# Last attention block of a two-layer convolutional attention kernel: denominators on 64 rows, reciprocals from PSUM, and the range check split over the last two blocks

## The chip, the core and the metric

The kernel runs on one core of one Trainium2 chip. The metric is the device time of one execution in microseconds; the time of a kernel is the median of its runs. A profile is one execution recorded by the hardware profiler.

The engines in what follows: PE is TensorE (PEld its weight loads), DVE is VectorE, ACT is ScalarE, POOL is GpSimd, and SP issues most DMAs (SPq is its queue). An engine runs its own instructions in program order, and waits on semaphores for the others.

## The reference

Input x is (16, 256, 32, 32) in float32: 16 images with 256 channels and n = 1024 positions. Two layers, each with weights of its own, do the same:

```
def layer(x, Wq, bq, Wk, bk, Wv, bv, rel_h, rel_w):
    xf = _gn(x).reshape(b, c, n)           # groups of two columns of the last axis, mean and variance over channels too
    q, k, v = (proj(W, bias) for ...)      # 256 x 256, then 4 heads of d = 64
    sim  = einsum('bhdi,bhdj->bhij', q, k)
    rel  = (rel_h + rel_w).reshape(heads, d, n)
    qpos = einsum('hdi,bhdj->bhij', rel, q)
    attn = softmax(sim + qpos, axis=-1)
    return einsum('bhdn,bhmn->bhdm', v, attn)

x = x + layer(x, L0...)
x = x + layer(x, L1...)
```

Two terms make the logits: sim, and the position term qpos. The softmax needs, for each head and each query i, the sum of 1024 exponentials: the denominator. The division by it is done after the product with v.

## The kernel before

**Tiling.** A unit is one image in one layer (32 units, the two layers interleaved). Its four heads are worked on as two pairs `pr`; a pair fills 128 partitions, 64 for each head. The 1024 queries are cut into two halves of 512. So there are 32 x 2 x 2 = 128 blocks (unit, pair, half), numbered 0 to 127. A block walks over eight slices `j` of 128 keys. With keys on the partitions, the logits of one slice are a PSUM tile of 128 x 2 x 512: two heads, 512 queries.

**One slice.** `seed` (L332) lets VectorE write the position terms into the PSUM tile: the products of rel with q were made once for each pair (`positions`, L309), and the seed adds the part of rel_h and the part of rel_w with broadcasts. `scores` (L348) adds the product of k and q on top with four matmuls of 64 x 64 x 512 (the trace has two records for each). They are quadrants of the array: the head picks the 64 rows, the half of the slice's keys picks the 64 columns. ACT takes the exponential into SBUF (L357). `add_up` (L366, L368) adds the eight results on VectorE into `acc`, so that `acc` still has to be summed over its 128 partitions.

**The rest of a block.** `attend` (L382) multiplies v with the exponentials into a PSUM tile `po`, in two stretches with a word from POOL (L152) between them. In the second half of a pair, `sums_of_p` (L405) sums the two `acc` of the pair over the partitions with matmuls against ones; each of the four (half, head) gets 32 rows of `po`. `take_out` copies `po` to SBUF (`od`; L417 in the first half, L422 in the second), and four DMAs (L431) take one row of each sum into `den_all`, where a block's denominators stand as 128 x 8. In the next block, `reciprocals` (L439) inverts them as 128 x 16, writes them to DRAM (L442) and reads them back, broadcast over 64 partitions a head, as `rden` (L445). `finish` multiplies (L456), adds bias and x (L457), and in layer 1 sends the result to `out` (L459).

**Order.** The whole is written under a manual schedule: each engine gets its instructions in the order of the program text. `block(n)` writes out that order by hand. Four PSUM tiles of two banks, `ring` = b, c, a, d, rotate; the seeds of slices 1 to 3 of the next block are made at the end of a block, between the stretches of `attend`. While a block runs, the projections, normalisation and position terms of the coming unit are put between its slices as `pieces` (`first`, `second`). The last two blocks, 126 and 127, have no such pieces.

**The end.** After block 127 come `reciprocals` and `finish` for the last pair. Then, outside the manual schedule, a pool of its own checks that every denominator lies between 1e-22 and 1e24: two operations and a reduction over `den_all` as 128 x 1024 (L969, L971, L973), a matmul that counts the good partitions (L975), and a cast to an integer (L977). The program reads this flag and branches: if a partition is out of range, a slow general path computes everything anew. The exponentials use a fixed shift instead of a maximum, which is why the check is there.

Of the kernel before, what the change touches and what calls it, by code (L numbers as in the profile page):

```python
# [9 lines left out]
F32 = mybir.dt.float32  # L10
F32R = mybir.dt.float32r
I32 = mybir.dt.int32
AF = mybir.ActivationFunctionType
ALU = mybir.AluOpType
AX = mybir.AxisListType
SYNC = mybir.DependencyInfo(mybir.DependencyClass.Sync, mybir.DependencyReason.DATA)

P = 128
HALF = 512
# [5 lines left out]
DEN_LO = 1e-22  # L25
# [18 lines left out]
def flat(ap):  # L44
    return ap.rearrange("p w h -> p (w h)")
# [4 lines left out]


@with_exitstack
def fast_path(ctx, tc, sh, x, layers, out, W, den_all, token):

# [282 lines left out]
        )  # L339
        seeds[blk, j] = ps  # L340

    def scores(blk, j):
        u, pr, half = blk
        ps = seeds.pop((blk, j))
        for h, hs in enumerate(QUARTERS):
            for x, c in enumerate(QUARTERS):
                j0 = j * P + x * D
                nc.tensor.matmul(  # L348
                    ps[c, h, :],
                    ks[u, pr][hs, j0 : j0 + D],  # L350
                    qs[u, pr][hs, half * HALF : (half + 1) * HALF],
                    start=False,
                    stop=True,
                    skip_group_check=True,
                )
        p = ppool.tile([P, 2, HALF], F32, tag="p", name=f"p_{u}_{pr}_{half}_{j}")
        nc.scalar.activation(p, ps, AF.Exp, bias=W.shift)  # L357
        probs[blk, j] = p
# [53 lines left out]
    def take_out(blk, po):  # L412

        u, pr, half = blk
        if half == 0:
            outs[u, pr] = opool.tile([P, 3, HALF], F32, tag="od", name=f"od_{u}_{pr}")
            nc.scalar.copy(  # L417
                outs[u, pr][:, 0, :].rearrange("p (a n) -> p a n", a=2), po[:, :, :QUART]
            )
            return  # L420
        od = outs[u, pr]
        nc.scalar.copy(  # L422
            od[:, 1:3, :].rearrange("p z (a n) -> p z a n", a=2),
            po.rearrange("p a (z n) -> p z a n", z=2),
        )
        R = P // 4
        n = index[blk]
        for x in range(2):
            for h in range(2):
                r0 = (2 * x + h) * R  # L430
                nc.sync.dma_start(  # L431
                    den_all[h * D : (h + 1) * D, n - 1 + x, :], od[r0 : r0 + 1, 2, :]
                )

    def reciprocals(u, pr):

        n = index[u, pr, 0]
        r8 = fpool.tile([P, 2, 8], F32, tag="r8", name=f"r8_{u}_{pr}")
        nc.vector.reciprocal(r8, den_all[:, n : n + 2, :])  # L439
        rd = dpool.tile([2, 2, HALF], F32, tag="rd", name=f"rd_{u}_{pr}")  # L440
        for x in range(2):
            nc.sync.dma_start(rd[:, x, :].rearrange("h (a b) -> h a b", b=8), r8[:, x, :])  # L442
        rdens[u, pr] = opool.tile([P, 2, HALF], F32, tag="rden", name=f"rden_{u}_{pr}")
        for h in range(2):
            nc.sync.dma_start(  # L445
                rdens[u, pr][h * D : (h + 1) * D],
                rd[h : h + 1].to_broadcast([D, 2, HALF]),
            )

    def finish(u, pr):  # L450
# [8 lines left out]
            nc.sync.dma_start(flat(out[b, pr * P : (pr + 1) * P]), xs)  # L459


    blocks = [(u, pr, half) for u in range(NU) for pr in range(CC) for half in range(NH)]
    for n, blk in enumerate(blocks):
        index[blk] = n
    BPU = CC * NH

    ring = ["b", "c", "a", "d"]

    def nothing(*_):
# [28 lines left out]
    def block(n):  # L498
        blk = blocks[n]
        u, b = divmod(n, BPU)  # L500
        half = blk[2]
        before = blocks[n - 2][:2] if half == 0 and n > 0 else None
        after = blocks[n + 1] if n + 1 < len(blocks) else None
        one, two = u + 1 < NU, u + 2 < NU

        pieces = u + 1 < NU or b < 2
        f0, f1, f2, f3 = ring

        if half == 1:
            add_up(blocks[n - 1], 7)  # L510
        for j in range(1, 4):
            scores(blk, j)
        if b == 2 and u + 3 < NU and units[u + 3][0] not in xt:
            load_x(units[u + 3][0])
        (first, first_out), (second, second_out) = prepare(u, b)
        first(0)
        if b == 0 and one:
            norm_apply(u + 1, range(0, 1))
        if b == 1 and two:
            norm_sums(u + 2, range(9, 11))  # L520
        seed(blk, 4, f1)
        scores(blk, 4)
        add_up(blk, 1)
        if half == 0:
            if before:
                reciprocals(*before)
            add_up(blk, 2)
        if b == 0 and one:
            norm_apply(u + 1, range(1, 5))
        if b == 1 and two:  # L530
            norm_sums(u + 2, range(11, 12))
        if b == 2 and two:
            norm_squares(u + 2, range(0, 5))
        second(0)
        if half == 1:
            second_out()
        first(1)
        first_out()
        seed(blk, 5, f0)
        scores(blk, 5)  # L540
        if half == 0:
            add_up(blk, 3)
            second(1)
            second_out()
        seed(blk, 6, f1)
        scores(blk, 6)
        if pieces and half == 0:
            ring[2:] = f3, f2
        seed(blk, 7, ring[2])
        scores(blk, 7)  # L550
        if half == 1:
            add_up(blk, 2)
            add_up(blk, 3)
        add_up(blk, 4)

        if after:
            seed(after, 0, f0)
        if before:
            finish(*before)
        if b == 0 and one:  # L560
            norm_apply(u + 1, range(5, 9))
        if b == 0 and two:
            norm_sums(u + 2, range(0, 2))
        if b == 1 and two:
            norm_sums(u + 2, range(12, G))
        if b == 1 and one:
            norm_apply(u + 1, range(9, 11))
        if b == 2 and two:
            norm_squares(u + 2, range(5, 11))
        po = psum2(ring[3], f"po_{n}")  # L570
        values_of_p = attend(blk, po)
        values_of_p(0)
        if two and half == 1:
            mean, mean_out = (norm_mean if b == 1 else norm_var)(u + 2, zeroed(f1, f"pm_{n}"))
            mean(0)
        if after:
            scores(after, 0)
        if two and half == 1:
            mean(1)
            values_of_p.word()  # L580
            mean_out()
        add_up(blk, 5)
        if half == 1:
            add_up(blk, 6)
            add_up(blk, 7)
        if after:
            for j in range(1, 4):
                seed(after, j, ring[j % 3])
        if half == 0:
            add_up(blk, 6)  # L590
        if b == 0 and two:
            norm_sums(u + 2, range(2, 9))
        if b == 1 and one:
            norm_apply(u + 1, range(11, G))
        if b == 2 and two:
            norm_squares(u + 2, range(11, G))
        values_of_p(1)
        if half == 1:
            sums_of_p(blocks[n - 1 : n + 1], po)
        take_out(blk, po)  # L600


    load_x(0)
# [107 lines left out]
    seed(blocks[0], 3, ring[0])  # L711
    for n in range(len(blocks)):
        block(n)
    reciprocals(*blocks[-1][:2])
    finish(*blocks[-1][:2])


@with_exitstack
# [224 lines left out]
def kernel(  # L943
# [10 lines left out]
    nblk = sh.NL * sh.B * sh.CC * sh.NH  # L954
    den_all = const.tile([P, nblk, 8], F32, tag="den_all", name="den_all")
    token = const.tile([1, 1], F32, tag="token", name="token")
    with tc.manual_schedule():
        W = Weights(tc, sh, layers, const)
        fast_path(tc, sh, x, layers, out, W, den_all, token)


    with ExitStack() as s:
        pool = s.enter_context(tc.tile_pool(name="chk", bufs=1))
        psum = s.enter_context(
            tc.tile_pool(name="chk_ps", bufs=1, space=bass.MemoryType.PSUM)
        )
        flatden = den_all.rearrange("p n e -> p (n e)")
        low = pool.tile([P, nblk * 8], F32, tag="low", name="low")
        nc.vector.tensor_scalar(low, flatden, DEN_LO, None, ALU.is_ge)  # L969
        good = pool.tile([P, nblk * 8], F32, tag="good", name="good")  # L970
        nc.vector.scalar_tensor_tensor(good, flatden, DEN_HI, low, ALU.is_le, ALU.mult)  # L971
        cnt = pool.tile([P, 1], F32, tag="cnt", name="cnt")
        nc.vector.tensor_reduce(cnt, good, AX.X, ALU.min)  # L973
        pc = psum.tile([P, 1], F32, tag="pc", name="pc")
        nc.tensor.matmul(pc[0:1, :], cnt, W.ones[:, 0:1], start=True, stop=True)  # L975
        flag = const.tile([1, 1], I32, tag="flag", name="flag")
        nc.vector.tensor_copy(flag, pc[0:1, :])  # L977
    ok = nc.values_load(flag[0:1, 0:1], min_val=0, max_val=P)
    with tc.If(ok < P):
        general_path(tc, sh, x, layers, out, W)  # L980
# [30 lines left out]
```

## Time and profile before

| what | value |
|---|---|
| median of three runs | 2654.65 us (2654.4 to 2658.43) |
| the profiled execution | 2655.58 us |
| its span on the core | 2652.5 us |
| mean granted TensorE clock | 0.995 |
| chain that ended last, by engine | PE 84%, DVE 6%, DMA 6%, SP's queue 2% |
| PE waiting at L348 for the seeds, all blocks | 15.1 us |
| VectorE waiting at L439 for den_all, all pairs | 39.6 us |
| VectorE waiting at L456 for rden, all pairs | 31.8 us |

The span is what the trace shows on the core; around it lie 3.1 us of the profiled execution. Busy times are sums over the span and can hide that stages have different limits, so the last 70 us are read by slices and by the timeline. A row of the timeline has the start, the duration, the engine, the line of the kernel, the operation, output<-input with shapes, the count, and in brackets the idle time ahead of it with what ended it. Rows of the groups have busy time, mean duration of one in ns, and the idle time ahead of the group with what ended it.

### The profile page before, as it was taken

Reading aid. Unit: us, or ns where it says so; the run is one execution under the profiler, and the core shown is the slowest. Engines: PE = TensorE matmul, PEld = TensorE weight load, DVE = VectorE, ACT = ScalarE, POOL = GpSimd, SP = SyncE. Lnnn points to the kernel's source line nnn. Section 1 sums busy time; section 2 is a strip of 40 time slices with the busy share of each in tenths; the row PEclk is TensorE's granted clock in tenths of the full one; section 3 lists DMA queues with packets and bytes.
Section 4 is the critical chain, followed back from the end, with each engine's and each line's share of the span. In section 5 each row is a group of like instructions: output and inputs, shape, how many; then the busy total and the mean of one; then the engine's idle time right before and its main releaser. Section 6 shows DMA issues by size and latency. Waiting matters only on the chain.

```text
span 2652.5 us, 86141 instructions
## 1 busy us (share of the span) xinstructions
PE 2591.0 (98%) x38406; PEld 1389.7 (52%) x38406; DVE 2423.2 (91%) x2198; ACT 1980.2 (75%) x3916; POOL 176.5 (7%) x450
## 2 busy tenths in 40 slices
PE   7999999999999999999999999999999999999994
PEld 3555555555555555555555555555555555555552
DVE  6999999999999999999999999999999999999996
ACT  5778777787777787777877777877778777778652
POOL 1000000000000000000000000000000000000000
PEclk9999999999999999999999999999999999999997
DMA  2010010101001010010100101001010100000001
GB/s 74 11 33 18 26 34 19 34 26 34 26 19 42 18 42 18 18 50 10 42 26 10 50 18 34 26 26 34 19 34 27 34 26 19 26 18 26 26 26 34
DMA packets 61499, 75.48 MB, mean 28 GB/s; under 512 B 43200, under 2 KB 44736, under 8 KB 61120
## 3 DMA queue, kind: packets, MB, share of 16 engines
q1 hardware_dynamic: 59664, 69.83, 9.1%
q8 instruction: 302, 4.95, 0.8%
q14 instruction: 77, 0.63, 0.1%
q10 hardware_dynamic: 1456, 0.07, 0.0%
HBM read 52.04 MB, written 17.30 MB: 26 GB/s over the span
## 4 chain that ended last, share of the span: by engine, by line
PE 84%; DVE 6%; DMA 6%; SPq 2%; issue 1%; ACT 1%; POOL 0%; DVEq 0%; POOLq 0%
PE po L382 30%; PE ps L348 29%; PE pv L281 7%; PE pq L251 7%; PE pk L251 7%; DVE ps L332 3%; PE po L405 2%; DMA rd<-r 2%; DMA rden<-rd 2%; PE pa L309 2%; DVE acc L368 2%; DMA den_all<-od 1%; SPq L431 1%; DVE x L457 1%; DVE od L456 1%
## 5 line engine op out<-in xcount | busy, mean ns | idle before, releaser
L357 ACT ACTIVATE p<-ps,shift 128x1024 f32<-128x1024 f32 x1024 | 1092.3, 1114 | 337.4 <-PE ps L348 215.4
L332 DVE TENSOR_TENSOR ps<-abt 128x1024 f32<-128x1024 f32 x1024 | 1228.7, 1228 | 112.3 <-ACT p L357 94.1
L348 PE MATMUL ps<-q,k 64*64 64x512 f32 x8192 | 997.5, 593 | 15.5 <-DVE ps L332 15.1
L368 DVE TENSOR_TENSOR acc<-acc,p 128x1024 f32<-128x1024 f32 x768 | 933.7, 1216 | 16.1 <-DVE r L439 0.2
L382 PE MATMUL po<-p,v 64*64 64x256 f32 x16384 | 933.1, 376 | 0.3 <-POOL token L152 0.3
L382 PEld LDWEIGHTS po<-p,v 64*64 64x64 f32 x16384 | 668.3, 133 | 294.6 <-issue 60.4
L348 PEld LDWEIGHTS ps<-q,k 64*64 64x64 f32 x8192 | 299.1, 133 | 443.3 <-issue 273.3
L251 PE MATMUL pq<-xn,Wq 64*64 64x512 f32 x2048 | 244.3, 592 | 4.0 <-DVE xn L640 4.0
L281 PE MATMUL pv<-Wv,xn 64*64 64x256 f32 x4096 | 244.3, 376 | 1.6 <-POOL token L152 1.3
L251 PE MATMUL pk<-xn,Wk 64*64 64x512 f32 x2048 | 242.8, 589 | 0.0
L231 ACT ACTIVATE xn<-x,nshift,rstd 128x128 f32<-128x128 f32 x501 | 213.4, 501 | 1.6 <-POOL nshift L654 1.6
L281 PEld LDWEIGHTS pv<-Wv,xn 64*64 64x64 f32 x4096 | 153.6, 133 | 103.3 <-issue 51.1
L176 ACT ACTIVATE junk<-x,neg 128x128 f32<-128x128 f32 x489 | 191.7, 399 | 0.0
L152 POOL MEMSET token<- 1x1 f32 x380 | 33.8, 89 | 2360.2 <-PE po L382 657.9
L422 ACT COPY od<-po 128x1024 f32<-128x1024 f32 x64 | 64.8, 1012 | 152.1 <-PE po L405 152.1
L366 DVE TENSOR_TENSOR acc<-p,p 128x1024 f32<-128x1024 f32 x128 | 155.9, 1218 | 0.0
L251 PEld LDWEIGHTS pq<-xn,Wq 64*64 64x64 f32 x2048 | 78.5, 134 | 145.6 <-issue 133.0
L176 ACT ACTIVATE junk<-x 128x128 f32<-128x128 f32 x480 | 144.9, 311 | 0.7 <-DVE x L457 0.7
L251 PEld LDWEIGHTS pk<-xn,Wk 64*64 64x64 f32 x2048 | 75.4, 133 | 124.2 <-issue 124.2
L220 POOL TENSOR_TENSOR rstd<-var,mhalf 128x16 f32<-128x16 f32 x30 | 113.2, 3773 | 59.1 <-ACT var L218 59.1
L456 DVE TENSOR_TENSOR od<-od,rden 128x1024 f32<-128x1024 f32 x64 | 78.2, 1221 | 31.9 <-DMA rden<-rd 31.8
L291 ACT COPY v<-pv 128x1024 f32<-128x1024 f32 x64 | 64.8, 1012 | 48.1 <-PE pv L281 48.1
(59 smaller groups left out, 921.1 us busy)
## 6 DMA issues: line engine op xcount, KB each, us to landing
rden<-rd SPq DMA_DIRECT2D x128, 256.0 KB
x<-in_x_dram SPq DMA_DIRECT2D x32, 512.0 KB
out_dram<-x SPq DMA_DIRECT2D x32, 512.0 KB
den_all<-od SPq DMA_DIRECT2D x256, 2.0 KB
rd<-r SPq DMA_DIRECT2D x128, 4.0 KB
raw<-in_L_conv_Wq_dram SPq DMA_DIRECT2D x2, 256.0 KB
raw<-in_L_conv_Wk_dram SPq DMA_DIRECT2D x2, 256.0 KB
raw<-in_L_conv_Wv_dram SPq DMA_DIRECT2D x2, 256.0 KB
```

Source lines behind the costliest of these rows:

```text
L176: nc.scalar.activation(junk, grouped(xt[units[u][0]], g), func, accum_out=into[:, g : g + 1], **bias)
L220: nc.gpsimd.tensor_tensor(rstd, var, W.mhalf[:, :G], ALU.pow)
L231: nc.scalar.activation(grouped(xns[u], g), grouped(xt[units[u][0]], g), AF.Identity, bias=shift[:, g : g + 1], scale=rstd[:, g : g + 1],)
L251: yield nc.tensor.matmul(pk[c, nh, :], w[l][rs, cc, c0 : c0 + D], xns[u][rs, cc, nh * HALF : (nh + 1) * HALF], start=(t == 0 and cc == 0), ...
L281: yield nc.tensor.matmul(pv[c, a, i, :], xns[u][rs, cc, j0 : j0 + D], W.wv[l][rs, cc, :], start=(t == 0 and cc == 0 and i == 0), stop=(t = ...
L332: nc.vector.tensor_tensor(ps.rearrange("p h (w y) -> p h w y", y=H), ab[:, :, :H].unsqueeze(2).to_broadcast([P, 2, XH, H]), ab[:, :, H + h ...
L348: nc.tensor.matmul(ps[c, h, :], ks[u, pr][hs, j0 : j0 + D], qs[u, pr][hs, half * HALF : (half + 1) * HALF], start=False, stop=True, skip_g ...
L357: nc.scalar.activation(p, ps, AF.Exp, bias=W.shift)
L366: nc.vector.tensor_tensor(accs[blk], probs[blk, 0], probs[blk, 1], ALU.add)
L368: nc.vector.tensor_tensor(accs[blk], accs[blk], probs[blk, j], ALU.add)
L382: yield nc.tensor.matmul(po[c, a, :QUART], vts[u][rs, j, c0 : c0 + D], p[rs, h, a * QUART : (a + 1) * QUART], start=(t == 0 and j == 0), s ...
L456: nc.vector.tensor_tensor(o, o, rden, ALU.mult)
```

## The change

- In `scores` the two loops change places: the key half is now the outer loop and the head the inner one, in all blocks.
- `widen`, called once, in block 125, adds rel_h and rel_w into one tile of 128 x 1024 (`wide`).
- Blocks 126 and 127 are written out in a function of their own, `block_without_pieces`. In both, slices 4, 5 and 6 get no seed: `scores` with a tag makes the position terms by a matmul of q with `wide` that starts the accumulation, followed by the matmul of k with q.
- Block 126's denominators no longer wait for those of block 127: after the first three slices of block 127 their sums are made, copied and sent to `den_all` on their own, and inverted as 128 x 8.
- In block 126, `in_range` checks the denominators of blocks 0 to 123 (992 columns), after `finish` of the pair before.
- In block 127, `sums_on_rows` makes the denominators on 64 rows for each head, which is how `po` needs them, in PSUM, ahead of the second stretch of `attend`. The reciprocal reads them from PSUM (128 x 512), and `finish_half` reads `po` from PSUM. `sums_on_columns` makes the same denominators as eight columns for the check. The first half's result leaves by `finish_half` too.
- Three ranges (992, 24 and 8 columns) are merged into one value for the count and the flag. The pool for the check goes.

```
@@ scores
-        ps = seeds.pop((blk, j))
-        for h, hs in enumerate(QUARTERS):
-            for x, c in enumerate(QUARTERS):
+        ps = psum2(tag, ...) if tag else seeds.pop((blk, j))
+        columns = slice(half * HALF, (half + 1) * HALF)
+        for x, c in enumerate(QUARTERS):
+            for h, hs in enumerate(QUARTERS):
                 j0 = j * P + x * D
+                terms = [(ks[u, pr], qs[u, pr])]
+                if tag:
+                    terms = [(qs[u, pr], wide[u, pr])] + terms
+                for i, (a, b) in enumerate(terms):
+                    nc.tensor.matmul(ps[c, h, :], a[hs, j0 : j0 + D], b[hs, columns],
+                        start=bool(tag) and i == 0, stop=i == len(terms) - 1, ...)
@@ new
+    def widen(u, pr):
+        r = W.rel[units[u][1]][:, pr, :]
+        t = gnpool.tile([P, CC, N], F32, tag="gn", ...)[:, 0, :]
+        nc.vector.tensor_tensor(..., ALU.add)
+        wide[u, pr] = t
...
+    def finish_half(u, pr, half, o, rden):
+        b, l = units[u]
+        columns = slice(half * HALF, (half + 1) * HALF)
+        xs = xt[b][:, pr, columns]
+        y = outs[u, pr][:, half, :]
+        nc.vector.tensor_tensor(y, o, rden, ALU.mult)
+        nc.vector.scalar_tensor_tensor(xs, y, W.bv[l][:, pr : pr + 1], xs, ALU.add, ALU.add)
+        nc.sync.dma_start(flat(out[b, pr * P : (pr + 1) * P])[:, columns], xs)
+
+    def in_range(den, i):
+        t = small.tile([P, den.shape[-1]], F32, ...)
+        nc.vector.tensor_scalar(t, den, DEN_LO, None, ALU.is_ge)
+        nc.vector.scalar_tensor_tensor(t, den, DEN_HI, t, ALU.is_le, ALU.mult)
+        nc.vector.tensor_reduce(good[:, i : i + 1], t, AX.X, ALU.min)
+
+    def sums_on_rows(acc, pd):
+        for h, c in enumerate(QUARTERS):
+            nc.tensor.matmul(pd[c, 0, :], W.ones[:, :D], acc[:, h, :], start=True, stop=True, ...)
+
+    def sums_on_columns(acc, pd):
+        for h in range(2):
+            for e in range(HALF // P):
+                nc.tensor.matmul(pd[:, 1, 4 * h + e : 4 * h + e + 1],
+                    acc[:, h, e * P : (e + 1) * P], W.ones[:, :1], start=True, stop=True, ...)
@@ block
+        if u + 1 == NU and b == 1:
+            widen(u, 1)
         f0, f1, f2, f3 = ring
+        if not pieces:
+            return block_without_pieces(n, half)
@@ new
+    def block_without_pieces(n, half):
+        blk = blocks[n]
+        u, pr, _ = blk
+        f0, f1, f2, f3 = ring
+        if half == 1:
+            add_up(blocks[n - 1], 7)
+        for j in range(1, 4):
+            scores(blk, j)
+        if half == 1:
+            po = pos[n - 1]
+            sums_of_p(blocks[n - 1 : n], po)
+            nc.scalar.copy(outs[u, pr][:D, 2, :]..., po[:D, :, QUART:])
+            keep_sums(outs[u, pr], n - 1, 1)
+        add_up(blk, 1)
+        seed(blk, 7, f2)
+        add_up(blk, 2)
+        reciprocals(*(blocks[n - 2][:2] if half == 0 else (u, pr, 1)))
+        add_up(blk, 3)
+        for j, tag in ((4, f1), (5, f0), (6, f1)):
+            scores(blk, j, tag)
+        scores(blk, 7)
+        add_up(blk, 4)
+        if half == 0:
+            seed(blocks[n + 1], 0, f0)
+            finish(*blocks[n - 2][:2])
+            in_range(flatden[:, : 8 * (n - 2)], 0)
+        po = pos[n] = psum2(f3, f"po_{n}")
+        values_of_p = attend(blk, po)
+        values_of_p(0)
+        if half == 0:
+            scores(blocks[n + 1], 0)
+        for j in (5, 6):
+            add_up(blk, j)
+        if half == 0:
+            for j in range(1, 4):
+                seed(blocks[n + 1], j, ring[j % 3])
+            values_of_p(1)
+            take_out(blk, po)
+            return
+        add_up(blk, 7)
+        acc = accs.pop(blk)
+        pd = psum2(f0, "pd")
+        sums_on_rows(acc, pd)
+        values_of_p(1)
+        sums_on_columns(acc, pd)
+        finish_half(u, pr, 0, outs[u, pr][:, 0, :], rdens[u, pr][:, 0, :])
+        rden = rdens[u, pr][:, 1, :]
+        nc.vector.reciprocal(rden, pd[:, 0, :])
+        finish_half(u, pr, 1, po[:, :, :QUART], rden)
+        in_range(flatden[:, 8 * (n - 3) : 8 * n], 1)
+        in_range(pd[:, 1, :8], 2)
+        nc.vector.tensor_reduce(good[:, 3:4], good[:, 0:3], AX.X, ALU.min)
+        pc = psum2(f1, "pc")[0:1, 0, 0:1]
+        nc.tensor.matmul(pc, good[:, 3:4], W.ones[:, 0:1], start=True, stop=True)
+        nc.vector.tensor_copy(flag, pc)
@@ after the loop over the blocks
-    reciprocals(*blocks[-1][:2])
-    finish(*blocks[-1][:2])
...
-        nc.vector.tensor_scalar(low, flatden, DEN_LO, None, ALU.is_ge)
-        nc.vector.scalar_tensor_tensor(good, flatden, DEN_HI, low, ALU.is_le, ALU.mult)
-        nc.vector.tensor_reduce(cnt, good, AX.X, ALU.min)
-        nc.tensor.matmul(pc[0:1, :], cnt, W.ones[:, 0:1], start=True, stop=True)
-        nc.vector.tensor_copy(flag, pc[0:1, :])
```

`keep_sums` holds the loop over DMAs that `take_out` had; `reciprocals` has got a `count` of halves.

More of the change, by code (lines that the diff above doesn't have):

```diff
@@ L52, in fast_path @@
 @with_exitstack
-def fast_path(ctx, tc, sh, x, layers, out, W, den_all, token):
+def fast_path(ctx, tc, sh, x, layers, out, W, den_all, token, good, flag):
     nc = tc.nc
@@ L340, in seed, with scores @@
         seeds[blk, j] = ps
-    def scores(blk, j):
+    wide = {}
+    def widen(u, pr):
+        r = W.rel[units[u][1]][:, pr, :]
+        t = gnpool.tile([P, CC, N], F32, tag="gn", name=f"wide_{u}_{pr}")[:, 0, :]
+        nc.vector.tensor_tensor(
+            t.rearrange("p (w y) -> p w y", y=H),
+            r[:, :H].unsqueeze(1).to_broadcast([P, sh.W, H]),
+            r[:, H:].unsqueeze(2).to_broadcast([P, sh.W, H]),
+            ALU.add,
+        )
+        wide[u, pr] = t
+    def scores(blk, j, tag=None):
         u, pr, half = blk
-        ps = seeds.pop((blk, j))
-        for h, hs in enumerate(QUARTERS):
-            for x, c in enumerate(QUARTERS):
+        ps = psum2(tag, f"ps_{u}_{pr}_{half}_{j}") if tag else seeds.pop((blk, j))
+        columns = slice(half * HALF, (half + 1) * HALF)
+        for x, c in enumerate(QUARTERS):
+            for h, hs in enumerate(QUARTERS):
                 j0 = j * P + x * D
[L348 to L355, printed above, removed]
+                terms = [(ks[u, pr], qs[u, pr])]
+                if tag:
+                    terms = [(qs[u, pr], wide[u, pr])] + terms
+                for i, (a, b) in enumerate(terms):
+                    nc.tensor.matmul(
+                        ps[c, h, :],
+                        a[hs, j0 : j0 + D],
+                        b[hs, columns],
+                        start=bool(tag) and i == 0,
+                        stop=i == len(terms) - 1,
+                        skip_group_check=True,
+                    )
         p = ppool.tile([P, 2, HALF], F32, tag="p", name=f"p_{u}_{pr}_{half}_{j}")
@@ L425, in take_out, with keep_sums @@
         )
+        keep_sums(od, index[blk] - 1, 2)
+    def keep_sums(od, n, count):
         R = P // 4
-        n = index[blk]
-        for x in range(2):
+        for x in range(count):
             for h in range(2):
@@ L431, in take_out, with reciprocals @@
                 nc.sync.dma_start(
-                    den_all[h * D : (h + 1) * D, n - 1 + x, :], od[r0 : r0 + 1, 2, :]
+                    den_all[h * D : (h + 1) * D, n + x, :], od[r0 : r0 + 1, 2, :]
                 )
-    def reciprocals(u, pr):
+    def reciprocals(u, pr, count=2):
         n = index[u, pr, 0]
         r8 = fpool.tile([P, 2, 8], F32, tag="r8", name=f"r8_{u}_{pr}")
-        nc.vector.reciprocal(r8, den_all[:, n : n + 2, :])
+        nc.vector.reciprocal(r8[:, :count, :], den_all[:, n : n + count, :])
         rd = dpool.tile([2, 2, HALF], F32, tag="rd", name=f"rd_{u}_{pr}")
-        for x in range(2):
+        for x in range(count):
             nc.sync.dma_start(rd[:, x, :].rearrange("h (a b) -> h a b", b=8), r8[:, x, :])
@@ L445, in reciprocals @@
             nc.sync.dma_start(
-                rdens[u, pr][h * D : (h + 1) * D],
-                rd[h : h + 1].to_broadcast([D, 2, HALF]),
+                rdens[u, pr][h * D : (h + 1) * D, :count, :],
+                rd[h : h + 1, :count, :].to_broadcast([D, count, HALF]),
             )
@@ L459, in finish @@
             nc.sync.dma_start(flat(out[b, pr * P : (pr + 1) * P]), xs)
+    def finish_half(u, pr, half, o, rden):
[7 more added lines that the diff above has]
+    def in_range(den, i):
+        t = small.tile([P, den.shape[-1]], F32, tag=f"range{i}", name=f"range{i}")
+        nc.vector.tensor_scalar(t, den, DEN_LO, None, ALU.is_ge)
[3 more added lines that the diff above has]
+        for h, c in enumerate(QUARTERS):
+            nc.tensor.matmul(
+                pd[c, 0, :], W.ones[:, :D], acc[:, h, :],
+                start=True, stop=True, skip_group_check=True,
+            )
+    def sums_on_columns(acc, pd):
+        for h in range(2):
+            for e in range(HALF // P):
+                nc.tensor.matmul(
+                    pd[:, 1, 4 * h + e : 4 * h + e + 1],
+                    acc[:, h, e * P : (e + 1) * P],
+                    W.ones[:, :1],
+                    start=True, stop=True, skip_group_check=True,
+                )
     blocks = [(u, pr, half) for u in range(NU) for pr in range(CC) for half in range(NH)]
@@ L465, in fast_path @@
     BPU = CC * NH
+    pos = {}
     ring = ["b", "c", "a", "d"]
@@ L546, in block @@
         scores(blk, 6)
-        if pieces and half == 0:
+        if half == 0:
             ring[2:] = f3, f2
@@ L600, in block @@
         take_out(blk, po)
+    flatden = den_all.rearrange("p n e -> p (n e)")
+    def block_without_pieces(n, half):
[9 more added lines that the diff above has]
+            sums_of_p(blocks[n - 1 : n], po)
+            nc.scalar.copy(
+                outs[u, pr][:D, 2, :].rearrange("p (a n) -> p a n", a=2), po[:D, :, QUART:]
+            )
+            keep_sums(outs[u, pr], n - 1, 1)
[19 more added lines that the diff above has]
+            add_up(blk, j)
+        if half == 0:
+            for j in range(1, 4):
[19 more added lines that the diff above has]
+        nc.vector.tensor_copy(flag, pc)
     load_x(0)
@@ L956 @@
     token = const.tile([1, 1], F32, tag="token", name="token")
+    good = const.tile([P, 4], F32, tag="good", name="good")
+    flag = const.tile([1, 1], I32, tag="flag", name="flag")
     with tc.manual_schedule():
         W = Weights(tc, sh, layers, const)
[L959 to L970, printed above, removed]
-        nc.vector.scalar_tensor_tensor(good, flatden, DEN_HI, low, ALU.is_le, ALU.mult)
-        cnt = pool.tile([P, 1], F32, tag="cnt", name="cnt")
-        nc.vector.tensor_reduce(cnt, good, AX.X, ALU.min)
[L974 to L977, printed above, removed]
+        fast_path(tc, sh, x, layers, out, W, den_all, token, good, flag)
     ok = nc.values_load(flag[0:1, 0:1], min_val=0, max_val=P)
```

## The prediction

> **What bounds the kernel now.** I read the busy shares first, then the chain of waits, then the slices of the last 70 us.
>
> ```profile
> span 2652.5 us, 86141 instructions
> PE 2591.0 (98%) x38406; PEld 1389.7 (52%) x38406; DVE 2423.2 (91%) x2198; ACT 1980.2 (75%) x3916; POOL 176.5 (7%) x450
> ```
>
> PE is busy 98% of the span: up to block 125 it is the bound, and what the change does there counts only through PE. The last two blocks differ. They have no projection pieces, so VectorE is full and PE waits; after the last attention both stand still (slices of 20, 20, 20 and 13 us; columns: length, busy us of PE, PEld, DVE, ACT, POOL, then PEclk, DMA share, GB/s):
>
> ```profile
> 2580.00:2600.00 20.00, 16.19 (x200) 6.69 (x196) 18.91 (x18) 8.99 (x10) 0.09 (x1) 0.91 0.12 29
> 2600.00:2620.00 20.00, 17.44 (x248) 8.41 (x240) 19.67 (x18) 10.09 (x10) 0.09 (x1) 1.00 0.07 27
> 2620.00:2640.00 20.00, 4.87 (x84) 2.77 (x80) 5.18 (x6) 1.01 (x1) 0.09 (x1) 0.72 0.11 28
> ```
>
> The timeline of the end:
>
> ```profile
> 2625.23 1.01 ACT L422 COPY od<-po 128x1024 f32<-128x1024 f32 x1 [7.27 <-PE po L405]
> 2626.27 2.42 SPq L431 DMA_DIRECT2D den_all<-od  x4
> 2630.00 0.25 DVE L439 RECIPROCAL r<-den_all 128x16 f32<-128x16 f32 x1 [6.78 <-DMA den_all<-od]
> 2638.05 1.23 DVE L456 TENSOR_TENSOR od<-od,rden 128x1024 f32<-128x1024 f32 x1 [7.80 <-DMA rden<-rd]
> 2643.37 0.69 DVE L969 TENSOR_SCALAR low<-den_all 128x1024 f32<-128x1024 f32 x1 [2.78 <-DMA out_dram<-x]
> 2646.91 0.15 DVE L977 CAST flag<-pc 1x1 int32<-1x1 f32 x1 [0.33 <-PE pc L975]
> ```
>
> Attention ends at 2624.1 and the span 28.4 us later: sums and copy 2.1, den_all round trip 3.8, reciprocal to rden 8.05, finish 2.6, output landing 2.7 (the checking pool waits for it), check 3.5, flag to end 5.6 (2646.91 to 2652.5).
>
> **The tail, part by part.** The round trips den_all and rden of the last block (together 11.8), the wait for the output (2.7) and the big check (3.2 of its 3.5) go; 5.6 after the flag stay. What stands there instead, from the end of the second attend stretch:
>
> 1. Eight column sums (sums_on_columns). Each loads 128x128 weights for one column; no such row exists. Nearest: the L648 loads, 107 ns apart, two passes each at full clock, so 8 x 2 x 107 = 1.7 us plus a drain of some 0.2: **1.9**. The reciprocal waits for PE's count, which stands behind them in program order, so it cannot run under the second stretch, though its own input is ready earlier.
> 2. The 128x512 RECIPROCAL from PSUM. Nearest rows:
>
> ```profile
> L439 DVE RECIPROCAL r<-den_all 128x16 f32<-128x16 f32 x64 | 16.2, 253 | 41.2 <-DMA den_all<-od 39.6 <-issue 1.6
> L699 DVE TENSOR_TENSOR sum<-first_sums 128x16 f32<-128x16 f32 x1 | 0.2, 175 | 0.0
> ```
>
> At 16 columns it is 78 ns dearer than an addition. If that is a fixed cost, 512 columns take 0.77 us (a 128x512 addition is 0.68); if it is per element (78/16 = 4.9 ns beside the 1.04 of an addition), 0.16 + 512 x 5.9 ns = 3.2. The Trainium skill, "VectorE: DVE Perf Modes" (First, the fixed hardware budget), says that reciprocal divides iteratively with a repeat count of 8; read as 8 cycles an element at 0.96 GHz, an estimate from that page is 4.3 + 0.16 = 4.4, whereas for 16 columns it would give 0.29 against the measured 0.253. I take the row: **3.2**; the sum ends 2.4 earlier with 0.77 and 1.2 later with 4.4.
> 3. 128x512 product 0.68 and sum 0.74 with gaps: 1.6. Then seven check operations on 24, 8 and 3 columns at 0.19 plus gaps: 1.5. Then pc and flag 0.35, then 5.6.
>
> Sum: 1.9 + 0.1 + 3.2 + 1.6 + 1.5 + 0.35 + 5.6 = **14.2** instead of 28.4. The output DMAs (2.6 to land) lie beside the 7.4 us from the sum to the end; not on the path. Gain of the tail: 14.2.
>
> **Blocks 126 and 127, where much of it is given back.** I walked the changed order of every engine with the rows' durations (score group 0.86 issue, 1.03 to its end; stretch 3.45; exp 1.11; seed, sum and product 1.22; rec to rden 8.06). The same walk over the old order reproduces the trace within 0.1 us.
>
> - widen, one 128x1024 operation (1.22) in block 125. VectorE has one hole of 0.78 there. Between 0 and 1.2 late: 0.5.
> - Six seeds fewer (6 x 1.14 = 6.8 of DVE). Their slices run twice the matmuls on PE: +0.86 each. PE had holes of 2.69 and 1.18 there, waiting for seeds.
> - Reciprocals of pair 124/125 stay in the early part of block 126, at 2593.7 (2592.2 before: a seed now stands ahead); rden lands 8.06 later, 2601.7. VectorE now reaches finish at 2597.4, since three seeds are gone: it **stalls 4.3 us**. Before, the same operation ran without a wait:
>
> ```profile
> 2600.23 1.22 DVE L456 TENSOR_TENSOR od<-od,rden 128x1024 f32<-128x1024 f32 x1
> ```
>
> Behind it in order: the range check of 992 columns (0.69 + 1.2 + 1.2 = 3.1), two sums, and seeds 1 to 3 of block 127.
> - Those seeds start at 2609.8 instead of 2603.83:
>
> ```profile
> 2603.83 3.50 DVE L332 TENSOR_TENSOR ps<-abt 128x1024 f32<-128x1024 f32 x3
> 2607.07 2.75 PE L348 MATMUL ps<-q,k 64*64 64x512 f32 x24
> ```
>
> PE is done with block 126 at 2604.4 and starts slice 1 of block 127 at 2611.1: **PE idles 6.7**.
> - The rule against the change: the Trainium skill, "TensorE: Matmul & The Clock Gate" (Why this matters for your kernels), wants no idle gap over some 3 us, since an idle window halves the clock. The trace agrees, with a hole of 2.69 already:
>
> ```profile
> 2594.70 1.98 PE L348 MATMUL ps<-q,k 64*64 64x512 f32 x8 [2.69 <-DVE ps L332]
> ```
>
> This score group took 1.98 instead of 1.09; the records of the clock stand at 0.5 for 3.4 us there. I price half clock until about 2615.2: **+1.4**. Without it the sum ends 1.4 earlier, with a second window 1.1 later.
> - Block 127: the 128x8 reciprocal waits some 1 to 2 us for den_all (copy 0.6, two DMAs 2.4); queued behind it are sums 3 to 7, so this is on the path. The sums on 64 rows (pd, 1.0) stand ahead of the second stretch on PE and need sum 7; before, that stretch began at 2620.5 while sum 7 ran until 2623.2. With DVE 1.9 later and the clock's 1.4, sum 7 ends at 2626.5, pd at 2627.6, attention at **2631.2** instead of 2624.1.
>
> So 7.1 comes back: 1.9 from VectorE (widen, stall, check and den_all wait, less six seeds), 3.8 from pd ahead of the stretch, 1.4 from the clock. Net 14.2 - 7.1 = 7.1; the walk gives a span of 2645.5, **7.0 less**.
>
> **Body.** The order of the four quadrant matmuls changes in all 1024 score groups. Two passes of 430 ns, each with all four quadrants at once, 7 ns apart: a group is 0.86 of pure streaming in any order, so I take 0. No trace shows the new order; bounds: 7 ns more a group is +7 us; below zero 115 ns a group stand between the 0.974 mean busy time of a group and its 0.86, of which I would credit at most 3 ns, 3 us. For the double matmuls the Trainium skill (same page, What overlaps and what doesn't) has a weight load overlap running matmuls only when its row group differs. Rows: loads of 133 ns are issued 2 ns after matmuls of the same rows begin, and groups lie 0.86 apart, so they do overlap. By rows 1.72 a slice; by the rule four loads more, 2.25, and the span ends at 2646.5.
>
> **Rivals.**
> - A, the tail's gain comes whole or nearly: reciprocal 0.77 (-2.4), no clock drop (-1.4), widen hidden (-0.3), or the stall shorter than walked. Together 2641.1 of span, some 11.4 gained, about 2643. For it: the hole sizes depend on landing times; against: rden landed 7.8 to 8.1 in every pair.
> - B, the double matmuls do not run four at a time but as pairs: 3.44 a slice, span 2650.05, 2.5 gained, 2652: no change. For it: no trace shows a group with two accumulating terms; against: attend accumulates over eight slices in the same quadrants without loss.
> - C, the other side: the new quadrant order costs at every switch, since consecutive matmuls now change rows each time instead of columns. To be slower by 0.2% it must eat 7.0 and add 5.3: 12.3/1024 = **12 ns a group** decides, visible as 600 ns or more instead of 593 in the scores row. At 15 ns: 2663. Against: the 7 ns spacing shows no such switch cost between rows now.
> - D, not what it says: the new flag, made of three ranges, sends the program into the general path, and the time is of another size; the ranges cover the same denominators, so nothing speaks for it.
>
> **How the numbers follow.** The profiled execution took 2655.58 (span 2652.5 plus 3.1), the median is 2654.65 (2654.4 to 2658.43), 0.93 less. 2655.58 - 7.0 = 2648.6 against that run; against the median 2647.6, and I give the latter. 0.2% (5.3 us) is about what a measurement of this kernel can tell from no change: faster is below 2649.3, slower above 2660. Forecast 0.5 (2645.5 to 2650, nine parts in ten of it faster), A 0.28, B and dear reciprocal or long half clock 0.14, C 0.06, D 0.02. Faster: 0.45 + 0.28 + 0.04 = 0.77; slower 0.07; the rest 0.16. The range goes from A's 2641.5 to B's far side, 2653.
>
> **What would show it.** VectorE idle some 4 us before the finish of pair 124/125, ended by rden; PE idle 6 to 7 before slice 1 of block 127, then half clock; RECIPROCAL 128x512 near 3.2, starting after the column sums; 14 us from the last attention matmul to the end; scores still 593 ns. Wrong would be: a stall under 2 us, a scores mean off by 10 ns, a doubled slice over 2 us, or attention ending before 2627.

## The result, and the profile after

| | before | after |
|---|---|---|
| median of six runs each | 2656.38 us (2653.53 to 2660.8) | 2646.69 us (2644.45 to 2648.23) |
| ratio | | 0.9962, 95% interval 0.9949 to 0.9975 |
| profiled execution, its span | 2655.58, 2652.5 | 2647.55, 2645.7 |
| last attend matmul ends, after it to the end | 2624.16, 28.3 us | 2631.80, 13.9 us |

The kernel is 0.38% faster (0.25% to 0.51%): some 10 us by the medians, 6.8 by the spans of the two profiled executions. Attention ends later than before, and what follows is half as long.

The slices of the changed kernel's last stretch, with the columns as in the prediction:

```profile
2580.00:2600.00 20.00, 19.95 (x276) 11.85 (x272) 17.25 (x16) 11.18 (x11) 0.09 (x1) 1.00 0.07 15
2600.00:2620.00 20.00, 13.86 (x159) 7.75 (x154) 15.87 (x14) 6.26 (x7) 0.09 (x1) 0.83 0.13 42
2620.00:2640.00 20.00, 13.47 (x182) 9.53 (x174) 13.39 (x18) 3.48 (x4) 0.09 (x1) 0.88 0.11 38
```

In the first slice PE is now full (19.95 of 20, 16.19 before) and VectorE no longer is. In the second both have holes and the granted clock is 0.83: a new wait. The timeline names it, and shows the new tail:

```profile
2602.64 1.22 DVE L478 TENSOR_TENSOR od<-od,rden 128x1024 f32<-128x1024 f32 x1 [4.35 <-DMA rden<-rd]
2603.90 1.28 DVE L479 SCALAR_TENSOR_TENSOR x<-od,bv,x 128x1024 f32<-128x1024 f32 x1
2605.11 0.67 DVE L496 TENSOR_SCALAR range<-den_all 128x992 f32<-128x992 f32 x1
...
2610.60 3.50 DVE L332 TENSOR_TENSOR ps<-abt 128x1024 f32<-128x1024 f32 x3
...
2611.88 4.21 PE L368 MATMUL ps<-q,k 64*64 64x512 f32 x24 [6.14 <-DVE ps L332]
...
2627.10 1.08 PE L503 MATMUL pd<-acc,ones 128*64 128x512 f32 x4 [0.29 <-DVE acc L388]
...
2628.11 3.69 PE L402 MATMUL po<-p,v 64*64 64x256 f32 x64
...
2631.72 1.95 PE L512 MATMUL pd<-ones,acc 128*128 128x1 f32 x16
2633.70 3.36 DVE L717 RECIPROCAL rden<-pd 128x512 f32<-128x512 f32 x1 [5.36 <-PE pd L512]
...
2640.13 0.15 DVE L724 CAST flag<-pc 1x1 int32<-1x1 f32 x1 [0.37 <-PE pc L723]
```

Read from the top: finish of pair 124/125 waits 4.35 us for rden; the check and two sums stand behind it in VectorE's order, and then the seeds that PE has been waiting for since 2605.7. PE's scores of slices 1 to 3 take 4.21 us instead of 2.75, for the most part at half clock. At the bottom, the reciprocal begins only when the last column sum is done.

### The profile page after: what moved, and what is told of

It reads as the page before. It is cut to its first block, busy times and chain, and to the rows that moved or that the text cites. A ratio compares the mean times of both kernels' runs of the same rounds, so it can differ in the third digit from the quotient of the medians.

```text
span 2645.7 us, 86265 instructions
## 1 busy us (share of the span) xinstructions
PE 2599.6 (98%) x38466; PEld 1403.0 (53%) x38466; DVE 2421.7 (92%) x2203; ACT 1980.3 (75%) x3916; POOL 176.1 (7%) x450
## 4 chain that ended last, share of the span: by engine, by line
PE 83%; DVE 7%; DMA 6%; SPq 1%; issue 1%; ACT 1%; POOL 0%; DVEq 0%; POOLq 0%; ACTq 0%
PE po L402 29%; PE ps L368 28%; PE pv L281 7%; PE pk L251 7%; PE pq L251 6%; DVE ps L332 3%; PE po L425 2%; DVE acc L388 2%; DMA rd<-r 2%; PE pa L309 2%; DMA rden<-rd 2%; DMA den_all<-od 1%; SPq L453 1%; DVE x L479 1%; DVE od L478 1%
## 5 line engine op out<-in xcount | busy, mean ns | idle before, releaser
L368 PE MATMUL ps<-q,k 64*64 64x512 f32 x8192 | 998.7, 594 | 14.6 <-DVE ps L332 14.3
```

The costliest lines, as they stand in the source:

```text
L368: nc.tensor.matmul(ps[c, h, :], a[hs, j0 : j0 + D], b[hs, columns], start=bool(tag) and i == 0, stop=i == len(terms) - 1, skip_group_check ...
```

## The experiments

The body in front of block 126 starts up to 3 us earlier or later from execution to execution (its sums lie at 2586.1 to 2589.3 in the eleven profiles here; in the changed kernel's profile the load of Wv at the start let PE go on 1.2 us later than in that of before). So spans are compared from one mark, the start of the sums of pair 124/125. In the kernel before and in the changed one these are:

```profile
2586.28 1.07 PE L405 MATMUL po<-acc,ones 128*32 128x256 f32 x16
...
2587.64 1.07 PE L425 MATMUL po<-acc,ones 128*32 128x256 f32 x16
```

Each row of the table is one profiled execution; the ratio is from medians, against runs of the kernel before taken along with it. The landing of rden alone moves a row by some 0.3 us: in the five kernels that have VectorE's stall ahead of finish, it is 4.03 to 4.40.

| kernel | mark to end of attention | attention to end | mark to end | ratio to before, 95% interval |
|---|---|---|---|---|
| before | 37.9 | 28.3 | 66.2 | |
| changed | 44.2 | 13.9 | 58.1 | 0.9962 [0.9949, 0.9975] |
| order of quadrants alone | 39.9 | 28.2 | 68.1 | 0.9997 [0.9988, 1.0005] |
| finish later | 40.9 | 13.7 | 54.6 | 0.9945 [0.9929, 0.9960] |
| check later | 41.4 | 13.9 | 55.2 | 0.9945 [0.9930, 0.9960] |
| columns apart | 43.9 | 8.9 | 52.8 | 0.9938 [0.9925, 0.9952] |
| rows behind | 43.3 | 14.7 | 58.0 | one run |
| seeds back | 52.4 | 13.9 | 66.3 | 0.9991 [0.9984, 0.9997] |
| PE kept busy | 43.0 | 14.4 | 57.4 | one run |
| together | 35.7 | 10.3 | 46.0 | 0.9920 [0.9907, 0.9934] |
| before, PE kept busy | 38.1 | 29.0 | 67.1 | 0.9994 [0.9985, 1.0002] |

**The order of the quadrants alone, on the kernel before.**

```
-        for h, hs in enumerate(QUARTERS):
-            for x, c in enumerate(QUARTERS):
+        for x, c in enumerate(QUARTERS):
+            for h, hs in enumerate(QUARTERS):
```

> The kernel before with only the two loops of scores exchanged. My theory: the body does not notice the order of the quadrants, a group stays at 0.86 us of streaming; scores row 593 to 594 ns, from the sums of pair 124/125 to the end of the span 66.2 us as before, ratio 1.000 within 0.0015, and about 3.1 us of the run lie outside the span as before. Rival (the new order is part of the gain, since the measured 9.7 us between medians exceed the 7.0 of the forecast): ratio 0.9985 to 0.999, 2.7 to 4 us less, and a mean of the scores row 1 to 2 ns lower.

Measured: ratio 0.9997 (0.9988 to 1.0005). Its group of scores:

```profile
L348 PE MATMUL ps<-q,k 64*64 64x512 f32 x8192 | 998.2, 594 | 14.4 <-DVE ps L332 13.7
```

The mean is 594 ns, as in the changed kernel, and 593 before. The interval leaves room for 3.2 us of gain and 1.3 of loss, and the group shows neither; that the order costs 12 ns a group, or carries the gain, is excluded. The mark to the end was not 66.2 as expected but 68.1, and the timeline shows where: in block 126 the clock dropped at another moment than in the profile of before, and two groups of scores took 3.69 us (2.50 before).

```profile
2594.57 1.09 PE L348 MATMUL ps<-q,k 64*64 64x512 f32 x8 [2.68 <-DVE ps L332]
...
2596.84 3.69 PE L348 MATMUL ps<-q,k 64*64 64x512 f32 x16 [1.18 <-DVE ps L332]
```

**Finish and check behind the seeds of block 127.**

```
             seed(blocks[n + 1], 0, f0)
-            finish(*blocks[n - 2][:2])
-            in_range(flatden[:, : 8 * (n - 2)], 0)
...
             for j in range(1, 4):
                 seed(blocks[n + 1], j, ring[j % 3])
+            finish(*blocks[n - 2][:2])
+            in_range(flatden[:, : 8 * (n - 2)], 0)
             values_of_p(1)
```

> The changed kernel with finish of pair 124/125 and the check of 992 columns moved behind the seeds of block 127's slices 1 to 3. Measure: from the sums of pair 124/125 to the end of the span (66.2 before, 58.1 changed). If the stall on rden is the root of what is given back (theory from the trace of the changed kernel): no idle time of VectorE ahead of finish, PE's hole ahead of slice 1 under 1 us, clock stays at 1.0 there, PE waits some 3 us for sum 7 of block 126 instead, and the measure falls by 5.2 to about 53. By the shares as the prediction gave them (1.9 for VectorE and 1.4 for the clock): it falls by 3.3 to about 54.8. Rival (PE is late for its own work, the stall is covered): it falls by less than 1.

Measured: 3.5 less instead of 5.2. The stall is gone, and PE reaches slice 1 without a hole:

```profile
2605.71 1.22 DVE L478 TENSOR_TENSOR od<-od,rden 128x1024 f32<-128x1024 f32 x1
...
2606.51 2.90 PE L368 MATMUL ps<-q,k 64*64 64x512 f32 x24
...
2612.57 1.74 PE L425 MATMUL po<-acc,ones 128*32 128x256 f32 x8 [3.15 <-DVE acc L388]
...
2614.24 2.00 PE L368 MATMUL ps<-wide,q 64*64 64x512 f32 x8
```

What is late next is sum 7 of block 126, now queued behind finish and check: PE waits 3.15 us for it. That wait was expected; that it would halve the clock again was not. The two groups after it take 1.74 and 2.00 instead of 1.06 and 1.11, and these 1.6 us are what is missing from the expected 5.2. The number hit the 3.3 of the prediction's shares, but not by their reasons.

**The check alone, moved behind the first half's product in block 127.**

```
             finish(*blocks[n - 2][:2])
-            in_range(flatden[:, : 8 * (n - 2)], 0)
...
         finish_half(u, pr, 0, outs[u, pr][:, 0, :], rdens[u, pr][:, 0, :])
+        in_range(flatden[:, : 8 * (n - 3)], 0)
```

> The changed kernel with only the check of 992 columns moved, from block 126 to block 127 behind the first finish_half, where VectorE stands idle for 5.4 us. Theory: finish still waits 4.3 us; PE's hole ahead of slice 1 of block 127 shrinks from 6.1 to about 3; the measure (sums of pair 124/125 to the end of the span, 58.1) falls by 3.2 if the clock still drops for a window and by 4.2 if it doesn't: about 54 to 55. Rival (the check lies under PE's second stretch anyway): less than 1 us.

Measured: 2.8 less; the hole is half of what it was, and still long enough for the clock:

```profile
2603.31 1.23 DVE L478 TENSOR_TENSOR od<-od,rden 128x1024 f32<-128x1024 f32 x1 [4.40 <-DMA rden<-rd]
...
2609.51 4.42 PE L368 MATMUL ps<-q,k 64*64 64x512 f32 x24 [3.17 <-DVE ps L332]
```

So the check's 3.1 us lay on the path nearly in full: in the changed kernel they were moved out of the tail and paid in block 126.

**The column sums in a PSUM tile of their own.**

```
-        sums_on_columns(acc, pd)
+        pe = psum2(f2, "pe")
+        sums_on_columns(acc, pe)
...
-        in_range(pd[:, 1, :8], 2)
+        in_range(pe[:, 1, :8], 2)
```

> The changed kernel with the eight column sums in a PSUM tile of their own, so that the reciprocal waits for the sums on rows alone. Theory: the reciprocal starts right after the row sums and runs under the second stretch of attend; from the end of the last attend matmul to the end of the span 14.0 falls to about 9; the measure from the sums of pair 124/125 falls by 5.0 to about 53. Rival (VectorE and PE disturb each other in PSUM, or the reciprocal waits for something else): it falls by less than 2, or the second stretch gets longer than 3.7 us by the same amount.

Measured: 5.3 less, 5.0 of it behind the attention (13.9 to 8.9); the other 0.3 is rden, which landed earlier here (a stall of 4.03 instead of 4.35):

```profile
2625.27 1.08 PE L503 MATMUL pd<-acc,ones 128*64 128x512 f32 x4 [0.29 <-DVE acc L388]
...
2626.28 3.69 PE L402 MATMUL po<-p,v 64*64 64x256 f32 x64
...
2626.89 3.35 DVE L718 RECIPROCAL rden<-pd 128x512 f32<-128x512 f32 x1
...
2629.90 1.95 PE L512 MATMUL pe<-ones,acc 128*128 128x1 f32 x16
```

The reciprocal runs beside the second stretch, and neither gets slower (3.35 and 3.69, as apart). In the changed kernel it waited for column sums that it doesn't read, because they share its tile: the order of the program is the same in both kernels.

**The sums on rows behind the second stretch.**

```
+        values_of_p(1)
         sums_on_rows(acc, pd)
-        values_of_p(1)
```

> The changed kernel with the sums on rows behind the second stretch of attend instead of ahead of it. The prediction put 3.8 us of what is given back on their place ahead of the stretch; if so, attention ends 3.8 earlier and, with 1.1 for the sums that now follow, the measure (sums of pair 124/125 to the end of the span, 58.1) falls by about 2.7. By the trace of the changed kernel PE waited only 0.29 us for sum 7 there: attention ends about 1.3 earlier, and the measure falls by 0.3, to about 57.8.

Measured, in one run: attention ends 0.9 earlier from the mark (2589.25 here), and the end comes 0.1 earlier. The prediction's 3.8 for their place is refuted.

```profile
2628.86 3.68 PE L402 MATMUL po<-p,v 64*64 64x256 f32 x64 [0.28 <-POOL token L152]
```

**The seeds back.**

```
         for j, tag in ((4, f1), (5, f0), (6, f1)):
-            scores(blk, j, tag)
+            seed(blk, j, tag)
+            scores(blk, j)
```

> The changed kernel with the position terms of slices 4 to 6 of the last two blocks seeded by VectorE again instead of made by matmuls. Theory: six seeds of 1.14 us come back on VectorE, the stall ahead of finish vanishes into them, PE's hole ahead of slice 1 of block 127 becomes about 2 us and the clock mostly stays, and the measure (sums of pair 124/125 to the end of the span, 58.1) rises by 4.0 to about 62. Rival (matmuls on PE cost what the seeds cost, so they gain nothing): within 1 us.

Measured: 8.2 more instead of 4.0; the ratio to the kernel before is then 0.9991, so little of the gain is left. The direction was right, the size not:

```profile
2596.92 3.69 PE L368 MATMUL ps<-q,k 64*64 64x512 f32 x16 [5.31 <-DVE ps L332]
...
2622.99 3.69 PE L368 MATMUL ps<-q,k 64*64 64x512 f32 x16 [5.65 <-DVE ps L332]
```

I had priced the seeds as VectorE work. In this order PE stands still for 5.3 and 5.65 us ahead of slices 4 and 5, once in each block, and the clock halves both times (two groups take 3.69 instead of 2.2). In this order the products are worth more than the six seeds that they save: they keep PE busy. The 8.2 us are the price of this order, though; the new end with the seeds placed earlier, as in the kernel before (holes of 0.84 and 2.69 us in block 126), was not tried.

**PE kept busy between blocks 126 and 127** (48 matmuls whose result is not used).

```
             take_out(blk, po)
+            for i in range(12):
+                for x, c in enumerate(QUARTERS):
+                    for h, hs in enumerate(QUARTERS):
+                        nc.tensor.matmul(po[c, h, QUART:], ks[u, pr][hs, x * D : x * D + D],
+                            qs[u, pr][hs, :QUART], start=True, stop=True, ...)
             return
```

> The changed kernel with 48 matmuls of 64x64x256 more between blocks 126 and 127, into columns of block 126's tile that its sums overwrite later; their result is not used. They fill some 5.2 of PE's 6.1 idle us and nothing waits for them. Theory: the clock stays at 1.0 through the scores of block 127's slices 1 to 3, these take 2.8 instead of 4.2 us, and the measure (sums of pair 124/125 to the end of the span, 58.1) falls by 1.1 to 1.4, to about 57. Rival (the clock's drop is hidden by VectorE's lag): less than 0.5.

Measured: attention ends 1.2 earlier from the mark. The whole is only 0.7 less, because 0.5 us more went by between the flag and the end of the span, a stretch that this kernel doesn't change (5.3 to 6.1 in ten of the profiles). The slice from 2608 to 2612 in the changed kernel and here (the granted clock, third from the right, is 0.50 and 1.00), and the scores of slices 1 to 3:

```profile
2608.00:2612.00 4.00, 0.12 (x4) 0.12 (x8) 3.90 (x5) 0.00 (x0) 0.00 (x0) 0.50 0.00 0
...
2608.00:2612.00 4.00, 3.98 (x76) 2.86 (x80) 3.86 (x5) 0.00 (x0) 0.00 (x0) 1.00 0.17 68
...
2613.25 3.34 PE L368 MATMUL ps<-q,k 64*64 64x512 f32 x24
```

They take 3.34, paced by the seeds, instead of 4.21. These 0.9 us are the clock's part; of the 1.2, some 0.3 come from VectorE, whose stall ahead of finish was 4.09 here instead of 4.35.

**All moves together.**

```
@@ block
+        if n in (32, 64, 96, 120):
+            m = (32, 64, 96, 120).index(n)
+            in_range(flatden[:, 8 * (0, 32, 64, 96)[m] : 8 * n], m)
@@ block_without_pieces, block 126
             for j in range(1, 4):
                 seed(blocks[n + 1], j, ring[j % 3])
+            add_up(blk, 7)
+            finish(*blocks[n - 2][:2])
@@ block 127
         add_up(blk, 4)
+            reciprocals(u, pr, 1)
...
         sums_on_rows(acc, pd)
         values_of_p(1)
-        sums_on_columns(acc, pd)
+        in_range(pd[:, 0, :], 4)
+        in_range(flatden[:, 8 * 120 : 8 * n], 5)
+        nc.vector.tensor_reduce(good[:, 6:7], good[:, 0:6], AX.X, ALU.min)
         finish_half(u, pr, 0, ...)
         nc.vector.reciprocal(rden, pd[:, 0, :])
+        nc.tensor.matmul(pc, good[:, 6:7], W.ones[:, 0:1], start=True, stop=True)
+        nc.vector.tensor_copy(flag, pc)
         finish_half(u, pr, 1, po[:, :, :QUART], rden)
```

> All moves together: finish of pair 124/125 behind the seeds and sum 7 of block 126; the check of the early denominators in four pieces of 192 to 256 columns after finish in blocks 32, 64, 96 and 120; the reciprocal of block 126 behind sum 4 of block 127; no column sums, the sums on rows are checked as 512 columns under the second stretch, the reciprocal runs there too, and the flag is cast ahead of the last product. Theory: attention ends about 8 us earlier, then about 9.5 us to the end; the measure (sums of pair 124/125 to the end of the span, 58.1) falls by 12 to 13, to about 45.5, and the pieces in the body cost nothing since VectorE has about 0.9 us of room a block there. Rival (the pieces of the check hold up PE in the body): the four blocks are longer by 1 us each, and 4 of the 12 us are lost.

Measured: 12.1 less from the mark, median 2636.76 us, ratio 0.9920 (0.9907 to 0.9934): it beats both kernels. PE's scores wait 8.8 us for seeds in the whole run (14.3 in the changed kernel). The pieces of the check are not free, as the theory had them, but they are far from the rival's 1 us each. The sums of the pairs with blocks 32, 64 and 96 follow those of the pair ahead after 40.43 to 40.45 us; in the ten other profiles it is 40.24 to 40.26, so such a piece costs 0.2 us. For block 120 it is 41.05 against 40.11 to 40.74: at least 0.3. Attention to end is 10.3 and not 9.5: the flag is cast 3.9 after attention, and 6.4 instead of 5.6 us follow it here; the last product, its sum and the output now stand behind the flag, but whether they make the difference was not tried. The three checks of 512 columns (0.69 each) and the first half's product stand ahead of the reciprocal, so that it comes out from under the stretch again; here more may be left to gain.

```profile
2620.68 3.68 PE L402 MATMUL po<-p,v 64*64 64x256 f32 x64
...
2620.80 0.69 DVE L496 TENSOR_SCALAR range<-pd 128x512 f32<-128x512 f32 x1 [1.55 <-PE pd L503]
...
2625.04 3.35 DVE L722 RECIPROCAL rden<-pd 128x512 f32<-128x512 f32 x1
```

**The kernel before with PE kept busy** (44 matmuls whose result is not used).

```
+        idle = psum2(f3, f"idle_{n}") if not pieces else None
...
+        kept_busy(2)
         scores(blk, 4)
...
+        kept_busy(5 if half == 0 else 2)
         scores(blk, 5)
```

> The kernel before with 11 groups of four matmuls of 64x64x256 more on PE in the holes of blocks 126 and 127 (2 ahead of slice 4 and 5 ahead of slice 5 in block 126, 2 and 2 in block 127), into a PSUM tile that nobody reads; nothing waits for them, and their results are not used. The question: the changed kernel's median is 10 us below the old one's, while the two profiled executions differ by 6.8. Theory: the old kernel's holes of 0.8 and 2.7 us in block 126 put the clock to half for one window or two, so that a typical run of it loses 2 to 3 us there, of which the profiled one (span 2652.5, the lowest of all seen) lost one; with PE kept busy the clock stays at 1.0 through block 127, the time from the sums of pair 124/125 to the end of attention is about 37, and the median is 2 to 3 us lower: ratio 0.9990. Rival (the runs differ at the start, by loads from DRAM, and the clock is no part of it): ratio 1.000, no less spread.

Measured: the clock stayed at 1.0 through blocks 126 and 127. In the slice below it stood at 0.73 before, and at 0.50 with the quadrants exchanged:

```profile
2596.00:2600.00 4.00, 2.29 (x20) 0.42 (x16) 4.00 (x5) 1.11 (x1) 0.00 (x0) 1.00 0.22 71
```

The stretch from the mark to the end of attention took 38.1 and not the 37 expected; that is what the profile of before has (37.9), with its shorter drop of the clock, and less than the 39.9 of the kernel with the quadrants exchanged. But the ratio is 0.9994 with 1 inside its interval, and the runs spread as widely. So a longer drop of the clock can cost some 2 us in one execution, as that one profile showed; that it costs a typical run 2 to 3 us is not confirmed, and the interval does not exclude it either.

## Why the prediction was right, point by point

**The total.** 2647.6 was predicted, the median is 2646.69; 7.0 less of span was predicted, and the two profiled executions differ by 6.8. From the mark to the end the gain is 8.1; widen took 0.3 of it ahead of the mark, and a body that was 1.05 late already before widen hides another 1.05. So what the forecast sums up is worth 7.8 in these two profiles, not 7.0. The medians differ by 9.7. Of the other 2.9, the time outside the span gives 1.2 (3.1 in the profile of before, 1.85 after), and 1.7 come from which executions were profiled: that of before lay 0.8 under the median of its six runs, that of the changed kernel 0.9 above. The prediction had no term for a change of either. 59 further runs of the kernel before had spans of 2652.7 to 2660.4, all longer than the 2652.5 that the sum started from; whether a typical run loses something in its last blocks that the profiled one did not is not settled. So it is in part luck that the median came within 1 us of the forecast, all the more as the forecast started from a median of three that lies 1.7 under the median of six.

**The tail** (predicted 14.2 in place of 28.4; measured 13.9 in place of 28.3). Column sums 1.9: 1.95. Reciprocal 3.2: 3.36. Its wait for the columns is there, but not for the reason given: the place of the columns in PE's order did not bind the reciprocal, the shared tile did (columns apart: 5.0 less). Of the three prices for the reciprocal, the one from the rows per element held, and the groups of the changed kernel (busy us, mean ns) show that it is linear:

```profile
L461 DVE RECIPROCAL r<-den_all 128x16 f32<-128x16 f32 x63 | 15.9, 253 | 35.3 <-DMA den_all<-od 33.8 <-issue 1.5
...
L717 DVE RECIPROCAL rden<-pd 128x512 f32<-128x512 f32 x1 | 3.4, 3358 | 5.4 <-PE pd L512 5.4
...
L461 DVE RECIPROCAL r<-den_all 128x8 f32<-128x8 f32 x1 | 0.2, 203 | 1.5 <-DMA den_all<-od 1.5
```

From 8 to 16 columns it is 50 ns, 6.25 a column; from 16 to 512 it is 3105 ns, 6.26 a column. The estimate from the eight repeats in the Trainium skill ("VectorE: DVE Perf Modes", First, the fixed hardware budget), 4.4, was too high by a third: the measurement decides.

**Blocks 126 and 127.** The stall was 4.35 (4.3 predicted), PE's hole 6.14 (6.7), and the clock dropped as the row of 2594.70 had suggested; keeping PE busy shows 0.9 of the 1.4. The 128x8 reciprocal waited 1.5 (1 to 2). widen moved the mark by 0.3 beyond what was late before it (0.5 predicted). A doubled slice issued in 1.72, loads and all:

```profile
2591.63 1.10 PE L368 MATMUL ps<-wide,q 64*64 64x512 f32 x8
...
2593.35 1.15 PE L368 MATMUL ps<-wide,q 64*64 64x512 f32 x8
```

Rival B (3.44) and the rule on weight loads in the Trainium skill ("TensorE: Matmul & The Clock Gate", What overlaps and what doesn't; 2.25) gave too much.

**Where it was wrong: the shares of what is given back.** "1.9 from VectorE, 3.8 from pd ahead of the stretch, 1.4 from the clock": the sum was nearly right (6.3 from the mark, and 0.3 for widen ahead of it), the split not. It compared sum 7 with the start of the second stretch, as if the stretch could have started at its old distance. By then the first stretch was 5.2 late already: it starts 30.3 after the mark before (2616.55) and 35.4 after (2623.07). The rows give: slice 1 of block 127 starts 24.2 instead of 20.8 after the mark, 3.45 for the wait on seeds; from there to the first stretch 11.2 instead of 9.5, 1.7 with the clock in it; from the first stretch to the end of attention 8.7 instead of 7.6, 1.1 for pd. Together 6.3. Moving pd gave attention 0.9, not 3.8; moving the check alone gave 2.8, moving finish and check 3.5 in spite of a new drop of the clock. The term that was mis-sized is VectorE's order in block 126: 1.9 in the prediction, and with 3.45 at slice 1 the larger part of the loss. The prediction led VectorE's delay to the end of attention through sum 7 and pd; it came mostly through PE's wait for the seeds.

**The body.** No effect to be seen, as taken; rival C needed 12 ns a group, and the row went from 593 to 594 ns.

## What to carry to other kernels

When work is moved out of a tail, look for what it queues ahead of: here an engine that runs in program order waited 4.35 us for a DMA, the check stood behind it, and PE's next scores, which needed the seeds behind both, started 3.45 us later. A tile shared by two products makes a reader of the one wait for the other; a tile of its own gave 5 us here. A split of a loss among causes is to be tested like the loss itself: take each cause away by itself.

## What the runs showed of the hardware that was not expected

The time outside the span was 1.8 to 3.5 us in the runs of the kernel before, and 1.75 to 1.9 in every kernel with the products in place of the seeds; with the seeds back and the new end it was 2.3 to 2.9. So it isn't the new end alone that shortens it. With PE kept busy in the kernel before, it was 1.8 to 3.1. The cause was not tried. A hole of PE of 3.15 us was enough for half clock (finish later), and so was one of 2.69 (before), while after one of 2.68 in the kernel with the quadrants exchanged the next group still took 1.09, and the two groups after that 3.69: the length of a hole alone does not tell which group pays.
